# Who adds the residual in the last stages of a sandwich layer: GpSimd row by row, or VectorE in one instruction

## The chip, the cores and the metric

The kernel runs on one core of a Trainium2 chip. The metric is the device time of one execution in microseconds. Before the change it is 695.41 us, the median of three runs (694.97 to 696.55).

A core has five engines that each work off their own queue in order: TensorE (PE in the profile; its weight loads are listed as PEld), VectorE (DVE), ScalarE (ACT), GpSimd (POOL) and SyncE (SP), which here only issues DMAs. Engines wait for each other by semaphores. Matmuls write PSUM; everything else lives in SBUF, 128 partitions wide, and in DRAM.

## What is computed

Two residual layers over 8 sequences of 512 tokens with 256 features: linear attention, and a mixture of 8 experts of which each token uses 2. Each layer is normed on both sides. Cut to what matters here, the second one is:

```python
def ffn(x, ...):
    flat = x.reshape(-1, d)
    ... # top 2 of 8 experts, with their weights in combine
    out = 0.5 * gelu(flat @ shared_W + shared_b)
    for e in range(8):
        h = gelu(flat @ W1[e] + b1[e])
        out = out + combine[:, e:e + 1] * (h @ W2[e] + b2[e])
    out = (out - mean(out)) * rsqrt(var(out) + 1e-5) * gamma + beta
    return out

x = x + layernorm(attn(layernorm(x)))
x = x + layernorm(ffn(layernorm(x)))     # this last sum is what the change is about
```

All arithmetic is in fp32.

## The kernel before

**Fronts.** For each sequence a front (`front`) runs the attention layer, the first norm of the second layer, the shared expert and the choice of experts. It leaves three things in DRAM: the residual `x1_d`, the shared expert's output `acc_d`, and the token rows, scattered to their experts' slots.

**Jobs.** The experts' work is a list of jobs (`routed`), each a run of 128 to 512 slots of one expert. A job has a first layer (matmuls `ph`, L837; ScalarE's Gelu `h`, L844), and a second one (matmuls `po`, L959, for each tile of 128 slots; VectorE adds the bias, L962, and multiplies by the token's weight, L966, into `y`). GpSimd then issues an indirect DMA that adds the 128 rows of `y` to `acc_d` (`add_rows`, L812). Jobs of 512 slots, a wide first layer, use seven products in place of eight (L879), with sums before (VectorE's `T`, L796; GpSimd's `S`, L809) and after (VectorE's `hw`, L905 to L912). The last two jobs are not scattered: their rows are gathered straight into the last sequence by matmuls (`fin`, L1045) and added by VectorE (L1049).

**Last stages.** When all of a sequence's rows are in `acc_d`, its last stage (`back`) brings it home. It is a generator of six steps, and a table (`plan`) written out by hand says after which piece of which job each step is issued:

1. SyncE loads `accb` from `acc_d` and `xb` from `x1_d`.
2. VectorE takes statistics of `accb` (`st_d`, L983; `mv_d`, L985), and GpSimd makes the factor `rs_d` (L365, L366).
3. VectorE norms `accb`, with gamma and beta (L989, L993).
4. VectorE takes statistics again (`st_e`, L375; `mv_e`, L377); GpSimd makes `rs_e` and `sh_e` (L365, L366, L381, L382, L998).
5. ScalarE applies them to `accb`, four instructions of 256 columns (L387), and GpSimd adds `accb` to `xb`, four more (L1008).
6. SyncE stores `xb` to the output.

The steps of sequences 0 to 2 lie under the jobs of 512 slots of experts 0 to 3, those of 3 and 4 under the later jobs of experts 4 to 7, those of 5 and 6 under the last jobs. The end is close: sequence 6's steps 5 and 6 and sequence 7's last ones are all issued after the same, last piece, in this order. Sequence 7 takes another way (`close`), which the change leaves as it is.

**Order.** TensorE, VectorE and ScalarE keep the order in which the program issues their work (`manual_schedule`). GpSimd's work and the DMAs that it issues are chained by `in_turn`, SyncE's DMAs by `move`. So each engine's queue is the program's order, and an instruction that waits holds all that stand behind it on its engine.

There is a second user of the helper `finish_rows`: a loop at the end of the program that recomputes tokens if the experts' slots overflow. With these inputs it doesn't run, and nor does the branch in front of it; all 28 instructions of L1008 in the trace belong to sequences 0 to 6.

Of the kernel before, what the change touches and what calls it, by code (L numbers as in the profile page):

```python
# [10 lines left out]
ALU = mybir.AluOpType  # L11
# [5 lines left out]
def kernel(  # L17
# [21 lines left out]
    nc = tc.nc  # L39
# [5 lines left out]
    NT = C // P  # L45
# [339 lines left out]
    def ln_apply(dst, src, stats, t):  # L385
        rs, sh = stats[0:2]
        nc.scalar.activation(  # L387
            dst, src, AF.Identity, scale=rs[:, t : t + 1], bias=sh[:, t : t + 1]
        )
# [584 lines left out]
            yield  # L974


    def finish_rows(tiles, xts, shift, name, on_pool):

        n = len(tiles)
        st = small.tile([P, NT, 6], F32, tag="st", name=f"st_d{name}", bufs=3)  # L980
        mv = small.tile([P, NT, 2], F32, tag="mvd", name=f"mv_d{name}", bufs=3)
        for t in range(n):
            nc.vector.bn_stats(st[:, t, :], tiles[t])  # L983
        for t in range(n):
            nc.vector.bn_aggr(mv[:, t, :], st[:, t, :])  # L985
        rs = rsqrt(mv[:, 0:n, 1], n, f"d{name}", 4.0 * LN_EPS)
        yield
        for t in range(n):
            nc.vector.scalar_tensor_tensor(  # L989
                tiles[t], tiles[t], mv[:, t, 0:1], fgam, ALU.subtract, ALU.mult  # L990
            )
        for t in range(n):
            nc.vector.scalar_tensor_tensor(  # L993
                tiles[t], tiles[t], rs[:, t : t + 1], fbet, ALU.mult, ALU.add
            )
        yield
        rs, sh, _ = ln_stats(tiles, f"e{name}")
        in_turn(nc.gpsimd.tensor_tensor(sh[:, 0:n], sh[:, 0:n], shift, ALU.add))  # L998
        yield
        for t in range(n):  # L1000
            if on_pool:
                in_turn(nc.gpsimd.tensor_scalar(
                    tiles[t], tiles[t], rs[:, t : t + 1], sh[:, t : t + 1], ALU.mult, ALU.add
                ))
                in_turn(nc.gpsimd.tensor_tensor(xts[t], xts[t], tiles[t], ALU.add))
            else:
                ln_apply(tiles[t], tiles[t], (rs, sh), t)
                in_turn(nc.gpsimd.tensor_tensor(xts[t], xts[t], tiles[t], ALU.add))  # L1008

    def back(b, in_order=True):  # L1010
        acc = act.tile([P, NT, D], F32, tag="acc", name=f"accb_{b}", bufs=4)
        last = len(adds)
        if in_order:
            first = [j[0:2] for j in jobs[: n_jobs - CLOSE] if j[1] < room(b, j[0])]
            last = max(ends[j] for j in first)
        ld = move(acc, rows_of(acc_d, b))
        unordered(ld, "acc", [fills[b], *adds[last - 1]])

        tag, bufs = ("acc", 4) if b < 3 else ("x", XB)
        xt = act.tile([P, NT, D], F32, tag=tag, name=f"xb_{b}", bufs=bufs)  # L1020
        move(xt, rows_of(x1_d, b))
        yield
        if b < B - 1 or not in_order:
            yield from finish_rows(
                [acc[:, t, :] for t in range(NT)], [xt[:, t, :] for t in range(NT)],
                shifts[:, b, :], f"{b}", False,
            )
            yield
            move(out[b].rearrange("(p t) d -> p t d", t=NT), xt)
        else:  # L1030
            yield from close(acc, xt)
# [319 lines left out]
    with tc.If(n_any > 0, preferred_fallthrough_block=False):  # L1351

        with tc.If(n_rest > 0, preferred_fallthrough_block=False):
            for k, y, one_w, _ in closing:
                nc.vector.tensor_scalar_mul(y, y, one_w)
                adds.append([add_rows(k, 0, y, adds[-1]).ins])
            jobs += [(E + m, CAP, CAP + P) for m in range(MORE, MOST)]
            for k in range(n_jobs, len(jobs)):
                biases_of(jobs[k][0] - E)
                load_w(jobs[k][0])  # L1360
                fetch(k)
                if k == n_jobs:
                    turn(k)
                fetch(k + 1)
                for _ in routed(k):
                    pass
            for _ in back(B - 1, in_order=False):
                pass

        out_flat = out.rearrange("b c d -> (b c) d")
        with tc.If(n_steps > 0, preferred_fallthrough_block=False):
            with tc.For_i(0, n_steps, 1) as u:
                xt = act.tile([P, NU, D], F32, tag="x", name="dx", bufs=XB)
                nc.sync.dma_start(
                    xt, x1_d[bass.ds(u * -U + (B * C - U), U), :].rearrange("(p t) d -> p t d", t=NU)
                )
                comb = small.tile([P, NU, E], F32, tag="wd", name="dcomb")
                nc.sync.dma_start(  # L1380
                    comb, comb_d[bass.ds(u * -U + (B * C - U), U), :].rearrange("(p t) e -> p t e", t=NU)
                )
                shift = small.tile([P, NU], F32, tag="sd", name="dshift")
                nc.sync.dma_start(
                    shift, shift_d[bass.ds(u * -U + (B * C - U), U), :].rearrange("(p t) o -> p (t o)", t=NU)
                )
                xn = act.tile([P, NU, D], F32, tag="xn", name="dxn", bufs=XN)
                stats = ln_stats([xt[:, t, :] for t in range(NU)], "dc")
                for t in range(NU):
                    ln_apply(xn[:, t, :], xt[:, t, :], stats, t)  # L1390
                xT = act.tile([P, ND, U], F32, tag="xT", name="dxT", bufs=4)
                transposed(xT, [xn[:, t, :] for t in range(NU)], "d")
                acc = act.tile([P, NU, D], F32, tag="y", name="dacc", bufs=2)
                for t in range(NU):
                    ps = bank(f"dpsh_{t}")[:, 0, :]
                    for i in range(ND):
                        nc.tensor.matmul(
                            ps, xT[:, i, t * P : (t + 1) * P], wsg[:, i, 0:D],
                            start=(i == 0), stop=(i == ND - 1),
                        )  # L1400
                    nc.vector.tensor_tensor(acc[:, t, :], ps, bsh, ALU.add)
                nc.scalar.activation(acc, acc, AF.Gelu)
                for e in range(E):
                    load_w(e, name="d")
                    hs = []
                    for c in range(NH):
                        ph = bank(f"dph_{e}_{c}")[:, 0, :]
                        for i in range(ND):
                            nc.tensor.matmul(
                                ph[:, 0:U], w1[e][:, i, c * P : (c + 1) * P], xT[:, i, :],  # L1410
                                start=(i == 0), stop=(i == ND - 1),
                            )
                        ht = act.tile([P, U], F32, tag="h", name=f"dh_{e}_{c}", bufs=10)
                        nc.scalar.activation(
                            ht, ph[:, 0:U], AF.Gelu, bias=cols[:, e * NH + c : e * NH + c + 1]
                        )
                        hs.append(ht)
                    for t in range(NU):
                        po = pair(f"dpo_{e}_{t}")[:, 0, 0:D]
                        for c in range(NH):  # L1420
                            nc.tensor.matmul(
                                po, hs[c][:, t * P : (t + 1) * P], w2[e][c],
                                start=(c == 0), stop=(c == NH - 1),
                            )
                        yd = act.tile([P, D], F32, tag="rT", name=f"dy_{e}_{t}", bufs=2)
                        nc.vector.tensor_tensor(yd, po, b2b[e], ALU.add)
                        nc.vector.scalar_tensor_tensor(
                            acc[:, t, :], yd, comb[:, t, e : e + 1], acc[:, t, :], ALU.mult, ALU.add
                        )
                for _ in finish_rows(  # L1430
                    [acc[:, t, :] for t in range(NU)], [xt[:, t, :] for t in range(NU)],
                    shift, "dd", True,
                ):
                    pass
                nc.sync.dma_start(
                    out_flat[bass.ds(u * -U + (B * C - U), U), :].rearrange("(p t) d -> p t d", t=NU), xt
                )
# [32 lines left out]
```

## Time and profile before

| What | Value |
|---|---|
| Median of 3 runs | 695.41 us |
| The profiled execution's own time | 696.92 us |
| Its span in the profile | 695.2 us |
| Mean granted clock of TensorE | 0.976 |
| VectorE, busy from 500 us on (of 196 us) | 127.94 us |
| GpSimd, busy from 500 us on | 96.14 us |
| L1008, GpSimd's residual adds | 28, of 722 to 1752 ns, median 1268 ns |
| First and last start of L1008 | 538.3 and 675.9 us |

Times in the profile count from the start of the span. A line of the timeline gives the start, the duration, the engine, the line of the program, the operation with output and inputs, and how many instructions were merged; in brackets stands how long the engine had been idle, and what released it. A line of the waits gives who waited for whom, the total in us, how many times, and the longest. TensorE's end times are modelled, and spans on GpSimd are rough.

The last stages' residual adds fall in these stretches of GpSimd: sequence 0 at 538.27 for 3.31 us, sequence 1 at 567.35 for 4.17, sequence 2 at 593.32 for 3.47, sequence 3 at 632.52 for 3.30, sequence 4 at 643.40 for 3.31, sequence 5 at 661.30 for 3.29, sequence 6 at 673.88 for 2.79. The stores follow at 541.61, 571.54, 596.82, 637.96 and 649.81 us for the first five.

### The profile page before, as it was taken

The numbers are of one execution on the slowest core, as the hardware profiler recorded it, in microseconds if no ns is written. First come the engines' busy times: TensorE is split into PE (matmuls) and PEld (weight loads), VectorE is DVE, ScalarE is ACT, GpSimd is POOL, SyncE is SP. The second block draws the span as 40 slices with busy tenths as digits, with TensorE's granted clock in tenths as the row PEclk, the third lists the DMA queues.
The fourth block names the chain that finished last, engine by engine and source line by source line (L and its number), as shares of the span: only waits on it lengthen the run. The fifth ranks groups of instructions, "written<-read, shape, count | busy, mean of one in ns | idle before, by whom it ended". The sixth has DMA issues, their size and how long they took to land. (4 is left out here: it accounts for less than half of the span.)

```text
span 695.2 us, 10360 instructions
## 1 busy us (share of the span) xinstructions
PE 652.5 (94%) x3387; PEld 571.5 (82%) x3387; DVE 374.0 (54%) x1226; ACT 239.9 (35%) x589; POOL 317.0 (46%) x445
## 2 busy tenths in 40 slices
PE   6998989998999999999999999999999999998980
PEld 4887877876988888999898888898988887888870
DVE  3657769774565441111126466353677978246475
ACT  4444443553353323222233132131414134223440
POOL 4312326776547772212144345242436572536562
PEclk9999998999999999999999999999999999999995
DMA  7996113242978859755455354262645649799641
GB/s 227 381 346 247 62 61 122 108 145 108 293 237 271 283 123 265 219 153 130 129 133 166 85 170 104 48 174 34 188 130 174 198 120 305 205 286 297 215 144 58
DMA packets 77817, 124.17 MB, mean 179 GB/s; under 512 B 10870, under 2 KB 55100, under 8 KB 77756
## 3 DMA queue, kind: packets, MB, share of 16 engines
q1 hardware_dynamic: 65324, 106.22, 46.3%
q0 software_dynamic: 12432, 17.21, 13.0%
q8 instruction: 29, 0.48, 0.3%
q14 instruction: 32, 0.26, 0.1%
HBM read 83.58 MB, written 39.83 MB: 178 GB/s over the span
## 5 line engine op out<-in xcount | busy, mean ns | idle before, releaser
L812 POOL DMA_INDIRECT acc_d<-y,xr x65 | 102.0, 1570 | 210.6 <-DVE y L966 169.9
L959 PE MATMUL po<-w,h 128*128 128x256 f32 x560 | 127.2, 383 | 2.8 <-ACT h L844 2.8
L837 PE MATMUL ph<-rT,w 128*128 128x128 f32 (+1 forms) x800 | 127.5, 317 | 0.0
L837 PEld LDWEIGHTS ph<-rT,w 128*128 128x128 f32 x800 | 116.5, 191 | 9.0
L959 PEld LDWEIGHTS po<-w,h 128*128 128x128 f32 x560 | 105.5, 192 | 16.7 <-ACT h L844 3.2
L959 PE MATMUL po<-w,hw 128*128 128x256 f32 x512 | 115.2, 382 | 0.0
L844 ACT ACTIVATE h<-ph,cols 128x128 f32<-128x128 f32 (+1 forms) x176 | 60.5, 414 | 142.5 <-PE ph L837 141.3
L959 PEld LDWEIGHTS po<-w,hw 128*128 128x128 f32 x512 | 95.3, 190 | 16.2 <-ACT hw L885 4.2
L962 DVE TENSOR_TENSOR y<-po,b 128x256 f32<-128x256 f32 x67 | 28.3, 422 | 149.1 <-PE po L959 148.8
L721 POOL DMA_INDIRECT xs<-xn,slot x64 | 65.1, 1017 | 21.4 <-issue 19.0
L879 PE MATMUL p<-T,S 128*128 128x256 f32 x192 | 52.2, 380 | 0.6 <-DVE hw L905 0.6
L885 ACT ACTIVATE hw<-hw,cols 128x512 f32<-128x512 f32 x64 | 42.7, 714 | 25.5 <-DVE hw L912 25.5
L408 DVE COPY rT<-pt_r 128x512 f32<-128x512 f32 (+2 forms) x22 | 10.5, 475 | 61.6 <-PE pt_r L397 61.6
L879 PEld LDWEIGHTS p<-T,S 128*128 128x128 f32 x192 | 36.3, 190 | 6.1 <-DVE hw L905 1.3
L900 ACT COPY p<-p 128x256 f32<-128x256 f32 x32 | 11.9, 372 | 84.5 <-PE p L879 84.5
L879 PE MATMUL p<-rT,w 128*128 128x256 f32 x128 | 38.1, 379 | 0.0
L608 PE MATMUL psh<-wsg,xfT 128*128 128x264 f32 x128 | 32.7, 413 | 0.0
L573 PE MATMUL py<-wm,xT 128*128 128x256 f32 x128 | 29.2, 380 | 1.7 <-DVE wm L564 1.5
L608 PEld LDWEIGHTS psh<-wsg,xfT 128*128 128x128 f32 x128 | 26.1, 207 | 4.7
L573 PEld LDWEIGHTS py<-wm,xT 128*128 128x128 f32 x128 | 23.8, 189 | 5.8 <-ACT acc L618 1.1
L905 DVE TENSOR_TENSOR hw<-p,p 128x512 f32<-128x512 f32 x32 | 22.1, 690 | 10.3 <-PE p L879 10.3
L879 PEld LDWEIGHTS p<-rT,w 128*128 128x128 f32 x128 | 24.3, 190 | 3.3
(222 smaller groups left out, 984.8 us busy)
## 6 DMA issues: line engine op xcount, KB each, us to landing
w<-in_L_ffn_W_dram SPq DMA_DIRECT2D x50, 1024.0 KB, 6.9
xs<-pad SPq DMA_DIRECT2D x8, 1060.0 KB, 15.4
xr<-xs SPq DMA_DIRECT2D x26, 265.0 KB, 3.0
x<-in_L_attn_x_dram SPq DMA_DIRECT2D x8, 512.0 KB, 4.5
x_d<-x SPq DMA_DIRECT2D x8, 512.0 KB, 2.9
acc_d<-acc SPq DMA_DIRECT2D x8, 512.0 KB, 2.7
accb<-acc_d SPq DMA_DIRECT2D x8, 512.0 KB, 4.3
xb<-x_d SPq DMA_DIRECT2D x8, 512.0 KB, 5.0
```

The costliest lines, as they stand in the source:

```text
L573: nc.tensor.matmul(py[:, t, :], xT[:, i, tt * P : (tt + 1) * P], wm[:, i, 0:D], start=(i == 0), stop=(i == ND - 1),)
L608: nc.tensor.matmul(ps[:, t, 0 : D + E], xT[:, i, tt * P : (tt + 1) * P], wsg[:, i, :], start=(i == 0), stop=(i == ND - 1),)
L721: ins = in_turn(nc.gpsimd.indirect_dma_start(out=xs[:, :], out_offset=bass.IndirectOffsetOnAxis(ap=slot[:, t, j : j + 1], axis=0), in_=row ...
L812: ins = in_turn(nc.gpsimd.indirect_dma_start(out=acc_d[:, :], out_offset=bass.IndirectOffsetOnAxis(ap=xrs[k][t][:, DX - 1 : DX].bitcast(I3 ...
L837: nc.tensor.matmul(ph[:, (c - c0) * cs : (c - c0 + 1) * cs], w1[e][:, i, c * P : (c + 1) * P], rT[:, i, :], start=(i == 0), stop=(i == ND ...
L844: nc.scalar.activation(ht, ph[:, (c - c0) * cs : (c - c0 + 1) * cs], AF.Gelu, bias=(cols[:, e * NH + c : e * NH + c + 1] if e < E else b1m ...
L879: nc.tensor.matmul(dst, s(g), t, start=True, stop=True)
L885: nc.scalar.activation(part, part, AF.Gelu, bias=cols[:, c : c + 1])
L900: nc.scalar.copy(p1, p15[:, 0, :])
L905: nc.vector.tensor_tensor(h[:, 0:4:3, :], p26, p1.unsqueeze(1).to_broadcast(shape2), ALU.add)
L959: nc.tensor.matmul(po, h[t], w2[e][c], start=(n == 0), stop=(n == NH - 1),)
L962: nc.vector.tensor_tensor(y[:, t % CT, :], po, b2b[e], ALU.add)
```

## The change

Step 5 loses GpSimd's four adds and ends with ScalarE's apply. Step 6 begins with one VectorE instruction that adds all 1024 columns of `accb` to `xb`, and the store waits for it. In the loop that doesn't run here, the apply moves from GpSimd to ScalarE and the add from GpSimd to VectorE.

```diff
-    def finish_rows(tiles, xts, shift, name, on_pool):
+    def finish_rows(tiles, shift, name):
...
         for t in range(n):
-            if on_pool:
-                in_turn(nc.gpsimd.tensor_scalar(
-                    tiles[t], tiles[t], rs[:, t : t + 1], sh[:, t : t + 1], ALU.mult, ALU.add
-                ))
-                in_turn(nc.gpsimd.tensor_tensor(xts[t], xts[t], tiles[t], ALU.add))
-            else:
-                ln_apply(tiles[t], tiles[t], (rs, sh), t)
-                in_turn(nc.gpsimd.tensor_tensor(xts[t], xts[t], tiles[t], ALU.add))
+            ln_apply(tiles[t], tiles[t], (rs, sh), t)
...
             yield from finish_rows(
-                [acc[:, t, :] for t in range(NT)], [xt[:, t, :] for t in range(NT)],
-                shifts[:, b, :], f"{b}", False,
+                [acc[:, t, :] for t in range(NT)], shifts[:, b, :], f"{b}"
             )
             yield
+            nc.vector.tensor_tensor(xt, xt, acc, ALU.add)
             move(out[b].rearrange("(p t) d -> p t d", t=NT), xt)
```

The instructions of TensorE and ScalarE keep their order. On VectorE the new instruction of each sequence stands where step 6 is issued. For sequences 0, 1 and 2 that is behind the third `y` (L962, L966) of the job under which it lies; for 0 and 1 the next sequence's `st_e` comes next. Sequence 3's stands right behind `mv_e` of sequence 4, sequence 4's behind the `y` of expert 6's last job. Sequence 5's stands between the `y` of the second last job and `st_e` of sequence 6. Sequence 6's stands behind its own `mv_e` and ahead of the first two L1049, the last job's picks and its `y`.

## Prediction

> **What bounds the kernel now.** I read the page's engine table first, then the chain of waits, then TensorE's waits from 500 us on (the last stages lie there), then the timelines around each residual add.
>
> ```profile
> PE 652.5 (94%) x3387; PEld 571.5 (82%) x3387; DVE 374.0 (54%) x1226; ACT 239.9 (35%) x589; POOL 317.0 (46%) x445
> ...
> PE po L959 <- ACT h L844: 2.8, 1, 2.8
> PE fin L1045 <- DVE y L962: 2.2, 2, 1.7
> PE p L879 <- DVE hw L905: 0.6, 1, 0.6
> ```
>
> TensorE is busy 94% of the span, and the chain of waits only covers the last 2.3 us, on VectorE. So the adds matter in three places only: the three waits of TensorE above (after 500 us it has no others of weight), and the tail after its last matmul, where VectorE alone sets the end. GpSimd's 46% is no limit by itself.
>
> **The price of an add.** VectorE's two-input adds out of SBUF: 422 ns for 256 columns (the T rows, L796), 692 ns for 512 (the xb row, L1083). Slope 270 ns for 256 columns, so 1024 columns: 692 + 2 x 270 = 1.23 us, and the next instruction starts about 0.08 us before it ends (L1083 started 685.60, its follower 686.21), so 1.15 us in a queue. Seven of them: 8.6 us of VectorE. They replace 28 GpSimd adds of 1.27 us median, in seven stretches of 2.8 to 4.2 us, 23.6 us together. Nothing waits for those sums but the stores; what counts is whom each engine keeps waiting.
>
> **Sequences 0 and 1** (expert jobs with wide first layers). VectorE stalls while GpSimd adds: L966 at 539.95 took 1.80 us instead of 0.35; in sequence 1 the four L989 at 567.38 took 3.56 us and the four L993 2.12 us, against 1.66 and 1.66 in sequence 0. Rebuilt from sequence 0's start-to-start times, VectorE goes from the first L989 to the first hw add of the next job in 8.55 us. Without GpSimd's adds, but with the new one (1.2 us) in that stretch, sequence 0 reaches hw at 540.2 + 8.55 + 1.2 = 549.95 (before: 550.21), sequence 1 at 567.38 + 8.55 + 1.2 = 577.1 (before: 578.18). TensorE waited there for hw, 0.2 us and 0.65 to 0.8 us. I take **-0.9 us**; bounds: nothing gained, and +1.2 us each if the stall stays.
>
> **Sequence 2.** The add comes ahead of a job with a narrow first layer; VectorE idles 2.6 us per output tile there (L962 waits for po). Nothing. Without that cover it would cost 1.15 us of VectorE.
>
> **SyncE's queue, sequences 0 to 2.** The store moves from GpSimd's end (541.6, 571.5, 596.8) to VectorE's add (about 547.6, 575.0, 600.6), and what is queued behind it moves too: the first-layer weights of experts 4, 5, 6 by 6, 3.4 and 3.8 us, and a dozen loads behind the second. Experts 4, 5, 6 use those weights at 601.8, 616.0 and 630.1, some 29 us or more after the new issue, and a 1 MB weight lands in 6.9 us; the nearest other user is the gathered rows for the job of 594.4, issued at 584.3, perhaps 3 us later, landing within 3 to 6 us. Nothing; at the other end some 2 us if the DMA engines, 0.9 to 1.08 busy from 600 to 636, pass it on.
>
> **Sequences 3 and 4: the recovered stall.**
>
> ```profile
> 631.00 5.11 DVE L989 SCALAR_TENSOR_TENSOR accb<-accb,mv_d,fgam 128x256 f32<-128x256 f32 x4
> ...
> 632.52 3.30 POOL L1008 TENSOR_TENSOR xb<-xb,accb 128x256 f32<-128x256 f32 x4
> ...
> 641.64 2.07 ACT L387 ACTIVATE accb<-accb,sh_e,rs_e 128x256 f32<-128x256 f32 x4 [6.28 <-POOL sh_e L998]
> ...
> 644.02 5.41 PE L959 MATMUL po<-w,h 128*128 128x256 f32 x16 [2.75 <-ACT h L844]
> ```
>
> And one microsecond of the table of windows, whose field after the five engines' busy times is the granted clock:
>
> ```profile
> 646.00:647.00 1.00, 1.00 (x3) 0.74 (x3) 0.00 (x0) 0.08 (x1) 0.72 (x2) 0.50 0.98 285
> ```
>
> Read downwards, GpSimd's adds for sequence 3 hold VectorE's fourth L989 of sequence 4 (3448 ns instead of 477), so sequence 4's mean and variance come 3.45 us late, GpSimd's shift after them, ScalarE's apply after that; the job's Gelus are queued behind the apply, and TensorE idles 2.75 us. Then its clock is 0.50, from 645.1 to 648.5, and 16 matmuls take 5.41 us instead of 3.62. Layer starts of these jobs lie 7.25 us apart (630.07, 637.32); the next came at 649.27, so this place costs 11.95 - 7.25 = 4.7 us.
>
> After: the L989s and what follows end 3.45 us earlier, mv_e at 635.85. There the new add of sequence 3 starts (its inputs are long there) and GpSimd wants to read mv_e. Here a rule speaks against the change. The rows: a GpSimd scalar op of 0.23 us took 0.42 to 0.91 us beside VectorE's two-input ops, so +0.7 at most. The Trainium skill, SBUF — State Buffer, "Who interferes with whom": a VectorE instruction with two SBUF inputs contends with a GpSimd instruction that reads SBUF, and the second to issue blocks until the first is through. By that, GpSimd waits 1.1 us for the add. The apply then starts 2.35 us later (as 639.29 to 641.64): 638.9 by the rows, 639.3 by the rule; ends 641.0 or 641.4; the first Gelu is ready 0.3 us later, and TensorE wants it at 641.27. Stall 0.05 or 0.45 us. I take the rule's, since the 3448 ns row shows such a block in full: recovered **S = 4.25 us**, ends 3.8 and 4.7. Next gates: expert 8's weights (asked for at 624.9) and the rows of the last jobs, released by an indirect add that itself goes out 3 us earlier. None looks late.
>
> **Sequence 4's add**: VectorE idles 9.4 us. Nothing.
>
> **Tail: sequences 5 and 6.**
>
> ```profile
> 668.73 0.42 DVE L962 TENSOR_TENSOR y<-po,b 128x256 f32<-128x256 f32 x1
> 669.06 1.40 DVE L375 BATCH_NORM_STATS2 st_e<-accb 128x6 f32<-128x256 f32 x4
> ...
> 670.65 1.27 DVE L1049 TENSOR_TENSOR accb<-fin,accb 128x512 f32<-128x512 f32 x2
> ...
> 673.20 2.07 ACT L387 ACTIVATE accb<-accb,sh_e,rs_e 128x256 f32<-128x256 f32 x4 [4.44 <-POOL sh_e L998]
> 673.88 2.79 POOL L1008 TENSOR_TENSOR xb<-xb,accb 128x256 f32<-128x256 f32 x4 [0.71 <-ACT accb L387]
> 674.68 0.42 DVE L962 TENSOR_TENSOR y<-po,b 128x256 f32<-128x256 f32 x1 [1.85 <-PE po L959]
> ...
> 675.16 1.99 PE L1045 MATMUL fin<-y,pick 128*128 128x256 f32 x8 [0.52 <-DVE y L962]
> ```
>
> Before, the adds of sequence 6 ran on GpSimd beside everything. In VectorE's new order, add 5 stands between the first y and st_e, and add 6 straight after mv_e, ahead of the two L1049, the picks, the second y, and so of the last fin matmuls. Add 6 must wait for ScalarE's apply, which needs GpSimd, which needs mv_e: a round trip inside an in-order queue. From st_d of sequence 6 (before 661.41; after 661.41 - 4.25 - 0.3 for an indirect add landing sooner = 656.9): GpSimd no longer holds rs_d, so L993 starts at +3.4 instead of +4.8, the first y at +5.9 = 662.8; add 5 at 663.15; st_e 664.3; mv_e done +1.67 = 665.97; apply +2.42 to 668.4, done 670.5; add 6 at 670.55; L1049 x2 671.7; picks 672.9; second y 673.8 to 674.25; fin at **674.3**. By TensorE's shift alone fin would be at 675.16 - 4.25 = 670.9: the round trip costs **3.4 us**, and fin starts 0.86 us earlier than before.
>
> **The clock after that wait.** TensorE now idles from the end of po (668.8) to 674.3: 5.5 us. The trace: 2.75 us of idling brought 3.4 us at 0.50; 1.67 us brought none. The Trainium skill, TensorE: Matmul & The Clock Gate, "Why this matters for your kernels", warns of gaps over about 3 us. By it all 1.99 us of fin run at half speed, +2.0; by the trace, where the slow stretch was 3.4 us long and may have begun inside the gap, +1.0 to +1.9. I take **+1.5**; ends 0 and 2.
>
> **Sum.** fin: -0.86 - 0.9 + 1.5 = -0.3 us; all behind it (the last sums, norms and store) is as before. Against the profiled execution, 696.92 us (span 695.2 and 1.7 around it): 696.6. The median is 695.41, lowest 694.97. The 1.5 us between may be the half-clock stretch: it depends on where the idle gap falls in the window (the clock gate page, Part 1: the 3.4 us window runs free). Then a median run has less to recover, and 696.6 stands; if the difference is something else, 695.41 - 0.3 = 695.1. I lean to the former: **696.2 us**, own range 694.3 to 697.6.
>
> **Rivals.**
> - *The round trip decides* (slower): the tail cost, 3.4 + 1.5 us, is paid in full and S is not got: a weight or a row load is next in line, or the apply still comes late. Net 4.9 - 0.9 - S, so slower by over 0.2% once S is under 2.6 us. With S = 1: 698.4. For: the cost in the tail follows from the order of the queue, the gain from a chain of four engines. Against: no wait on DMA shows in those jobs.
> - *Relief decides* (faster): clock not halved in the tail, the rows of sequence 6 landing 1 us sooner, no block of GpSimd at 635.9: -0.3 - 1.5 - 0.7 - 0.4 = -2.9, 693.3 with half of the profiled offset. For: each is within its bounds; against: all are needed.
> - *VectorE in the wide stages* (slower): the stalls at 539.95 and 567.38 have another cause; two adds of 1.2 us delay hw and TensorE, +2.4 instead of -0.9: 699. Against: VectorE's long instructions end with GpSimd's adds each time.
>
> **Chances.** Forecast 0.45, round trip 0.26, relief 0.19, wide stages 0.10. A change below 0.2% (1.4 us) can't be told from none here. Forecast's share: same 0.30, slower 0.11, faster 0.04; round trip: slower 0.24, same 0.02; relief: faster 0.16, same 0.03; wide: slower 0.08, same 0.02. So faster 0.20, same 0.37, slower 0.43. Range 693.3 to 699.8: the two outer cases' times, and a little over for two costs together.
>
> **What would show it.** L989 of sequence 4 at 1.7 us in all, with no TensorE wait and no 0.50 clock near 644; hw waits near 550 and 578 gone; add 6 waiting some 4 us for ScalarE's apply, fin waiting for y by 5 us, a clock of 0.50 in the last fin. An L989 still of 3 us, or fin not waiting, would prove me wrong.

## The result, and the profile after

The changed kernel takes 700.95 us (median of 8 runs), the kernel before 697.52 us (8 runs beside them): the ratio is 1.0047, with a 95% interval from 1.0025 to 1.0069. The change makes the kernel slower by 1.7 to 4.8 us. The forecast of 696.2 us, and its range up to 699.8, are missed; that the median of before is itself 2.1 us higher than in the first three runs explains part of the miss in us, but not that the forecast's sum of -0.3 us came out as +3.4. The profiled execution took 703.92 us (span 702.2), the longest of the eight.

The changed kernel's page, its row of busy times:

```profile
PE 652.4 (93%) x3387; PEld 571.3 (81%) x3387; DVE 373.3 (53%) x1233; ACT 240.5 (34%) x589; POOL 299.9 (43%) x417
```

And its waits of TensorE from 500 us on (who waited for whom, total us, times, longest):

```profile
PE fin L1038 <- DVE y L962: 5.9, 2, 5.5
PE po L959 <- ACT h L844: 3.1, 2, 2.9
PE pt_r L397 <- DMA xr<-xs: 1.5, 1, 1.5
```

VectorE and GpSimd are both less busy than before, and the kernel is slower: what counts is TensorE's waits. The wait for hw is gone as forecast. But three waits of weight stand where there were three before: one for the gathered rows is new, the one at po has moved, and the one at fin has grown. In the order of the timeline:

**A new wait for the gathered rows.** SyncE's queue and TensorE, first before, then after:

```profile
571.54 0.34 SPq L129 DMA_DIRECT2D out_dram<-xb  x1
...
584.33 6.83 SPq L129 DMA_DIRECT2D xr<-xs  x2
...
594.44 0.60 PE L397 MATMUL pt_r<-identd,xr 128*128 128x128 f32 x4
```

```profile
576.89 0.34 SPq L129 DMA_DIRECT2D out_dram<-xb  x1
...
590.48 0.93 SPq L129 DMA_DIRECT2D xr<-xs  x2
...
597.32 0.63 PE L397 MATMUL pt_r<-identd,xr 128*128 128x128 f32 x4 [1.54 <-DMA xr<-xs]
```

The store of sequence 1 goes out at 576.89 (before 571.54), directly behind VectorE's add, and the loads behind it move with it: the rows xr (the first of the two merged loads) from 584.33 to 590.48. Before, they landed 7.5 us after their issue, 2.6 us ahead of their use. Now they land 6.7 us after it, and TensorE asks for them at 595.8, only 5.3 us after it.

**The stall of sequence 4, gone.** VectorE, GpSimd and TensorE:

```profile
633.91 1.67 DVE L989 SCALAR_TENSOR_TENSOR accb<-accb,mv_d,fgam 128x256 f32<-128x256 f32 x4
...
638.67 1.19 DVE L1021 TENSOR_TENSOR xb<-xb,accb 128x1024 f32<-128x1024 f32 x1
...
638.93 1.03 POOL L365 TENSOR_SCALAR rs_e<-mv_e 128x4 f32<-128x4 f32 x1 [2.99 <-DVE mv_e L377]
...
644.37 3.72 PE L959 MATMUL po<-w,h 128*128 128x256 f32 x16 [0.19 <-ACT h L844]
```

The four L989 take 1.67 us instead of 5.11, the wait at po is 0.19 instead of 2.75 us, and the sixteen matmuls run at full clock. GpSimd's first op on mv_e does block beside the new add: it takes 1.03 us instead of 0.23 and ends 0.10 us behind the add.

**A stall of the same kind, one sequence later.** SyncE, GpSimd and VectorE before:

```profile
649.38 0.33 SPq L129 DMA_DIRECT2D xr<-xs  x1
...
650.56 1.57 POOL L812 DMA_INDIRECT acc_d<-y,xr  x1 [3.85 <-DVE y L966]
...
653.97 1.67 DVE L993 SCALAR_TENSOR_TENSOR accb<-accb,rs_d,fbet 128x256 f32<-128x256 f32 x4 [0.54 <-POOL rs_d L366]
```

GpSimd, VectorE, ScalarE and TensorE after; the last line is that of L812 from 500 us on, the 23 semaphore waits of GpSimd's queue for indirect adds (shortest, median and longest in ns):

```profile
642.61 1.66 POOL L812 DMA_INDIRECT acc_d<-y,xr  x1 [0.66 <-issue]
652.66 1.56 POOL L812 DMA_INDIRECT acc_d<-y,xr  x1 [8.39 <-DVE accb L989]
653.70 0.81 POOL L365 TENSOR_SCALAR rs_d<-mv_d 128x4 f32<-128x4 f32 x1
...
655.67 1.67 DVE L993 SCALAR_TENSOR_TENSOR accb<-accb,rs_d,fbet 128x256 f32<-128x256 f32 x4 [3.58 <-POOL rs_d L366]
...
661.35 2.07 ACT L387 ACTIVATE accb<-accb,sh_e,rs_e 128x256 f32<-128x256 f32 x4 [2.99 <-POOL sh_e L998]
...
663.73 1.99 PE L959 MATMUL po<-w,h 128*128 128x256 f32 x8 [2.88 <-ACT h L844]
...
L812 POOLq EVENT_SEMAPHORE  x23: 17/43/9499, 511.1 to 661.2; - x23
```

Expert 7's rows y are ready at 648.9 (before 650.3), but their indirect add is issued at 652.66. The program lets a job's indirect adds wait for those of the job before it (`done` in `add_rows`), and this one waits until expert 6's, issued at 642.61, has landed at 651.93: that is the queue's wait of 9.50 us, and SyncE's next load of rows, held by the same landing, goes out at 651.98. The name in the bracket, L989, is only the event that came last by the profile; the adds do not read what L989 writes. Behind the add in GpSimd's queue stands rs_d of sequence 5, whose input was ready at 650.5. So VectorE idles 3.58 us before L993 instead of 0.54, sequence 5's chain comes 3.0 us late, its apply stands ahead of the second last job's Gelus, and TensorE waits 2.88 us.

Before, the same landing let SyncE's load go at 649.38, 0.9 us ahead of expert 7's rows, so their add had nothing to wait for. The landing hardly moves when the add is issued sooner. Counted from the first layer of expert 4's last job, the add was issued 40.5 us on in the four executions without sequence 3's change (before, e12, e1, e3) and landed 47.5 to 47.8 us on; in the eleven with it, it was issued 37.9 us on and landed 46.2 to 47.2 us on. Issued 2.6 us sooner, it landed 0.9 us sooner in the mean.

**The tail.** VectorE and TensorE, and two microseconds of the table of windows (the field after the five engines is the granted clock):

```profile
676.88 1.23 DVE L1021 TENSOR_TENSOR xb<-xb,accb 128x1024 f32<-128x1024 f32 x1 [4.52 <-ACT accb L387]
678.03 1.28 DVE L1042 TENSOR_TENSOR accb<-fin,accb 128x512 f32<-128x512 f32 x2
...
680.61 3.78 PE L1038 MATMUL fin<-y,pick 128*128 128x256 f32 x8 [5.47 <-DVE y L962]
```

```profile
678.00:679.00 1.00, 0.00 (x0) 0.00 (x0) 1.00 (x3) 0.45 (x2) 0.00 (x0) 1.00 0.05 20
...
681.00:682.00 1.00, 1.00 (x3) 0.78 (x3) 0.00 (x0) 0.00 (x0) 0.00 (x0) 0.50 0.00 0
```

The round trip is as forecast: add 6 stands 4.52 us in VectorE's queue waiting for ScalarE, everything behind it with it, and fin starts late, at half clock.

**The sum in the two traces.** From the first layer of expert 4's last job (601.78 before, 604.70 after) to the end of VectorE's last instruction it is 85.96 us before and 90.27 after: +4.31. In it are -4.26 (the first layer behind the recovered stall 43.23 us on instead of 47.49), +3.11 (from there to the last first layer: 17.63 instead of 14.52), +3.68 (from that to the last fin: 15.05 instead of 11.37) and +1.78 (from there to the end). Ahead of that stretch are -0.94 for sequences 0 and 1 and +1.54 for xr: +4.9 in all. VectorE ends 7.2 us later in all; of the 2.3 us left, 2.1 lie in the front, where nothing is changed.

### The profile page after: what moved, and what is told of

Its sections match the earlier page's. It is cut to its first block, busy times and chain, and to the rows that moved or that the text cites. A ratio compares the mean times of both kernels' runs of the same rounds, so it can differ in the third digit from the quotient of the medians.

```text
span 702.2 us, 10331 instructions
## 1 busy us (share of the span) xinstructions
PE 652.4 (93%) x3387; PEld 571.3 (81%) x3387; DVE 373.3 (53%) x1233; ACT 240.5 (34%) x589; POOL 299.9 (43%) x417
## 5 line engine op out<-in xcount | busy, mean ns | idle before, releaser
L812 POOL DMA_INDIRECT acc_d<-y,xr x65 | 104.4, 1606 | 221.1 <-DVE y L966 167.2
L962 DVE TENSOR_TENSOR y<-po,b 128x256 f32<-128x256 f32 x67 | 28.3, 422 | 140.7 <-PE po L959 140.7
L573 PE MATMUL py<-wm,xT 128*128 128x256 f32 x128 | 30.9, 396 | 3.9 <-DVE over L673 2.2
L608 PE MATMUL psh<-wsg,xfT 128*128 128x264 f32 x128 | 29.9, 387 | 0.0
L608 PEld LDWEIGHTS psh<-wsg,xfT 128*128 128x128 f32 x128 | 24.1, 191 | 3.9
```

Source lines behind the costliest of these rows:

```text
L573: nc.tensor.matmul(py[:, t, :], xT[:, i, tt * P : (tt + 1) * P], wm[:, i, 0:D], start=(i == 0), stop=(i == ND - 1),)
L608: nc.tensor.matmul(ps[:, t, 0 : D + E], xT[:, i, tt * P : (tt + 1) * P], wsg[:, i, :], start=(i == 0), stop=(i == ND - 1),)
L812: ins = in_turn(nc.gpsimd.indirect_dma_start(out=acc_d[:, :], out_offset=bass.IndirectOffsetOnAxis(ap=xrs[k][t][:, DX - 1 : DX].bitcast(I3 ...
L962: nc.vector.tensor_tensor(y[:, t % CT, :], po, b2b[e], ALU.add)
```

## The experiments

Every ratio is against the kernel before, on the same chip. What the profiles give is told as single executions.

**Where in the sequences is the loss?** Three kernels keep GpSimd's adds for all sequences but some (`ON_POOL` names those that keep them):

```diff
+    ON_POOL = (0, 1, 2, 3, 4, 5)      # e1;  e2: (0, 1, 2, 4, 5, 6);  e3: (3, 4, 5, 6)
...
-            nc.vector.tensor_tensor(xt, xt, acc, ALU.add)
+            if b not in ON_POOL:
+                nc.vector.tensor_tensor(xt, xt, acc, ALU.add)
```

e1, sequence 6 alone:

> Only sequence 6's add is on VectorE, the other six stay on GpSimd. Round trip theory (VectorE waits for ScalarE's apply ahead of the last job's work): fin starts 3.9 us later (y at 669.15, mv_e 670.7, apply done 675.3, add 6, two L1049, picks, y: 679.05 against 675.16) and its matmuls run at half clock, +1.5 to 1.8: +5.4 to 5.7 us, a ratio to before of 1.0078 (1.006 to 1.009), more than the whole change. Rival (the loss comes from VectorE's extra work in the wide jobs, the tail hides its own): within 1 us of before.

Measured: 1.0081 (1.0059 to 1.0103). fin waits 4.27 us for y and then takes 3.78 us. By the medians the tail alone costs more than the whole change; the two intervals overlap.

e2, sequence 3 alone:

> Only sequence 3's add is on VectorE. Theory that the recovered stall moves on to sequence 5 because an indirect add lands late: the L844 stall near 644 shrinks from 2.75 us to 0.5 or less and the slow clock behind it goes, a stall of 2 to 3 us shows up some 16 us later, net -1 to -2 us, ratio 0.997 to 0.999. Rival (the stall is got back in full and only the tail gives it away in the changed kernel): -4.3 us, ratio 0.994. Second rival (GpSimd's adds do not hold VectorE): no change, with L989 still over 3 us.

Measured: 0.999 (0.997 to 1.0011). L989 is at 1.67 us, the stall of sequence 4 gone, and a new one stands in the trace:

```profile
652.64 3.72 PE L959 MATMUL po<-w,h 128*128 128x256 f32 x16 [0.19 <-ACT h L844]
671.31 3.64 PE L959 MATMUL po<-w,h 128*128 128x256 f32 x8 [2.19 <-ACT h L844]
```

With nothing but sequence 3's add changed, the recovered stall comes back one sequence later, here with a half clock too (3.64 us for 8 matmuls instead of 1.99). So relief that shows in full at its own place in the trace is hardly seen in the time.

e3, sequences 0 to 2 alone:

> Only sequences 0, 1 and 2 have their adds on VectorE. Theory: TensorE's waits for hw near 550 and 578 go, -0.9 us; the store of sequence 1, now later, holds a dozen loads, and the rows for expert 4's second job come late, +1.5 us: net +0.6 us, ratio 1.000 to 1.002, with a wait of pt_r for xr of 1 to 2 us. Rival (VectorE's extra work in the wide jobs is the loss): +2.4 us or more, 1.0035, with longer waits for hw.

Measured: 1.0 (0.9975 to 1.0025). The waits for hw are gone, and TensorE waits 1.47 us for xr: gain and cost in the same place.

**The tail, by moving the step.** e4 is the changed kernel with step 6 of sequence 6 a piece later, so behind the last y:

```diff
-    ... (6, (7, 9, 10, 11, 13, 13)), ...
+    ... (6, (7, 9, 10, 11, 13, 14)), ...
```

> The changed kernel with one number of the plan altered: step 6 of sequence 6 is issued one piece later, behind the last job's y, where VectorE waits 1.2 us for fin anyway. Round trip theory: fin no longer waits 5.5 us for y and runs at full clock, -5.5 us against the changed kernel, so 2 us below before, ratio 0.997 (0.995 to 0.999). Rival (the tail is not the cause): as the changed kernel, 1.0047.

Measured: 0.9984 (0.9963 to 1.0006), 0.6% under the changed kernel. fin's wait is 0.52 us, at full clock. What remains: waits of 2.73 us at po, of 1.68 for xr and of 1.57 at the first fin (before 1.67), and add 6, which now stands ahead of the last sums:

```profile
679.75 1.23 DVE L1021 TENSOR_TENSOR xb<-xb,accb 128x1024 f32<-128x1024 f32 x1 [1.59 <-ACT accb L387]
680.89 1.28 DVE L1042 TENSOR_TENSOR accb<-fin,accb 128x512 f32<-128x512 f32 x2
```

**The tail, by undoing it.** e10 is the changed kernel with sequence 6's adds back on GpSimd (`ON_POOL = (6,)`):

> The changed kernel with one part undone: the adds of sequence 6 back on GpSimd, in four parts at their steps of before; sequences 0 to 5 stay on VectorE. Theory (the round trip of add 6 through VectorE and ScalarE before the last y costs 3.7 us and the clock that falls in it 1.8 us, and add 6 also stands ahead of the last L1042s, 1.5 us): the wait for y before fin L1038 falls from 5.5 to under 1 us, fin L1038 takes about 2 us and not 3.8, and the time is 5.5 to 7 us under the changed kernel's: ratio to before about 0.9965. The wait of 2.8 us for h (L844) at po of sequence 5 and that of 1.5 us for xr stay. Rival (the loss of the changed kernel is in the adds of sequences 0 to 5): ratio as the changed kernel's, 1.0047.

Measured: 0.9964 (0.9949 to 0.998), as expected. TensorE's waits:

```profile
PE po L959 <- ACT h L844: 2.5, 2, 2.3
PE fin L1044 <- DVE y L962: 1.2, 2, 0.7
PE pt_r L397 <- DMA xr<-xs: 1.1, 1, 1.1
```

Undoing this one part turns the loss into a gain: without the tail the change is worth 2.5 us (1.4 to 3.6).

**The stall of sequence 5, by moving a step.** e5 (with e4's edit) issues sequence 5's statistics and rs_d a piece earlier, ahead of expert 7's indirect add; e6 (with e4's edit) issues its apply a piece later, behind the Gelus:

```diff
-    ... (5, (2, 5, 6, 7, 9, 11)), ...
+    ... (5, (2, 4, 6, 7, 9, 11)), ...     # e5
+    ... (5, (2, 5, 6, 7, 10, 11)), ...    # e6
```

> As e4, and the statistics of sequence 5 (step 2) are issued one piece earlier, so that on GpSimd its rs_d stands ahead of the indirect add of expert 7's last job. Theory (that add waits for the one before it to land, 9 us after its issue, and holds rs_d behind it on GpSimd, so the apply of sequence 5 comes late and holds the Gelus): the wait of po for h near 663 falls from 2.7 us to 0.3 or less, -2.5 us against e4, ratio to before 0.995. Rival (the apply is late for another reason: the load of accb, or ScalarE's own work): the wait stays over 2 us, ratio as e4, 0.998.

> As e4, and the apply of sequence 5 (step 5) is issued one piece later, behind all eight Gelus of its job on ScalarE, with its cause left as it is. Theory (the harm of a late apply is that Gelus are queued behind it): the wait of po for h near 663 goes, -2.7 us against e4, ratio to before 0.995, while rs_d of sequence 5 stays as late as in e4. Rival (something else holds the Gelus or po): no change from e4, 0.998.

Measured: e5 0.9977 (0.996 to 0.9994), e6 1.0001 (0.9985 to 1.0017). In both the stall at po is gone. In e5 the first fin waits 3.76 us in its place (1.57 in e4), and runs at half clock:

```profile
662.71 1.66 POOL L812 DMA_INDIRECT acc_d<-y,xr  x1 [3.50 <-DMA acc_d<-y,xr]
665.07 1.41 DVE L983 BATCH_NORM_STATS2 st_d<-accb 128x6 f32<-128x256 f32 x4 [7.26 <-DMA accb<-acc_d]
671.43 3.78 PE L1038 MATMUL fin<-y,pick 128*128 128x256 f32 x8 [3.76 <-DVE y L962]
```

Now it is sequence 6's load of acc_d that VectorE waits for, and that load waits for expert 7's indirect add. In e6 the first fin waits 1.70 us, about as long as in e4 and before, and a wait of 0.67 us for rT is new; from expert 4's last job to the last fin its trace is 1.9 us shorter than e4's, but the time shows no gain (on another chip), and why isn't settled. Two later pairs of kernels differ in e6's edit alone: from e7 to e8 and from e13 to e11 a wait of 2.3 to 2.4 us at po goes, and one of 2.0 to 2.1 us at the first fin comes, where there was none. So moving steps of sequence 5 passes the delay on; both expectations took it for a local one.

**The store of sequence 1.** e7 (with e4's edit) issues the stores of sequences 0 and 1 five pieces later, e9 (with e4's edit) that of sequence 1 alone; the add stays where it is:

```diff
             nc.vector.tensor_tensor(xt, xt, acc, ALU.add)
+            if b == 1:                    # e7: if b < 2
+                yield
             move(out[b].rearrange("(p t) d -> p t d", t=NT), xt)
...
         for n in (0, 1, 3, 4, 8, 10):
             at(*under[6 * b + n], b)
+        if b == 1:                        # e7: if b < 2
+            at(*under[6 * b + 15], b)
```

> As e4, and the stores of sequences 0 and 1 leave step 6 and are issued five pieces after their adds, so that SyncE has no store ahead of the weights and rows of the next jobs. Theory (the store that waits for VectorE's add holds those loads): the wait of pt_r for xr near 597 goes, -1.6 us against e4, ratio to before 0.996. Rival (the rows come late since the weights' transfers take long, whatever the order): the wait stays at 1 us or more, ratio as e4.

> The kernel of e4 (step 6 of sequence 6 a piece later), with the store of sequence 1 alone issued five pieces later; the store of sequence 0 stays where it is. Theory (the store of sequence 1 waits in SyncE's queue for VectorE's add and holds the loads of the gathered rows behind it): TensorE's wait of 1.7 us for xr at L397 is gone, 1.6 us less than e4, ratio to before about 0.996. Rival (the rows land late for another reason: traffic, or the indirect adds): a wait of 1 us or more for xr stays, ratio about 0.998 as in e4.

Measured: e7 1.0007 (0.9989 to 1.0024), e9 0.9956 (0.9937 to 0.9974). e7 doesn't answer the question: with store 0 moved behind it, the load of xb for sequence 2 takes a buffer that waits 16.4 us in SyncE's queue for VectorE's add of sequence 1, so the rows came late all the same (TensorE waited 2.31 us). In e9 the rows go out at 581.94, 9.8 us ahead of their use, and TensorE's waits are

```profile
PE po L959 <- ACT h L844: 2.0, 2, 1.8
PE fin L1040 <- DVE y L962: 0.7, 2, 0.5
```

No wait for xr, with the same load landing 7.0 us after its issue: it was the store in SyncE's queue that made the rows late. The ratio falls from e4's 0.9984 to 0.9956, but on another chip and with intervals that overlap, so what the wait cost in time is rough, some 2 us.

**Together.** e8 is e4, e6 and e7 in one; e11 has sequence 6 on GpSimd, e6's later apply and e9's later store; e13 is e11 without the later apply:

> All three together: add 6 a piece later, apply of sequence 5 a piece later, the stores of 0 and 1 later. If the three costs are separate, -5.5 - 2.7 - 1.6 us against the changed kernel and so 6 to 6.5 us below before: ratio 0.991 (0.989 to 0.993). If what is freed at one place is held at the next again, 0.994 to 0.997 with a new wait of TensorE after 660.

> Three parts together: the adds of sequence 6 on GpSimd as before, the others on VectorE; the apply of sequence 5 a piece later; the store of sequence 1 five pieces later. If the three costs are separate (tail 5.5 us, po of sequence 5 2.8 us, xr 1.5 us, and the gains of 0.9 and 4.25 us stay): ratio to before 0.991 to 0.995, faster than both kernels. If one cause stands behind the other (the stall of sequence 5 passes on to fin, as in e5 and e6): about 0.998, with a new wait of TensorE for y or rT in place of the ones removed.

> Two parts together: the adds of sequence 6 on GpSimd as before (e10), and the store of sequence 1 five pieces later (e9); sequence 5 stays as in the changed kernel. If the two costs are separate: TensorE's wait for xr is gone, fin starts without a long wait, ratio to before 0.994 to 0.9955, faster than both kernels, and faster than e11; the wait of about 2 us for h at po of sequence 5 stays. If taking the wait for xr away only lengthens the wait for h at po: 0.9964 as in e10.

Measured: e8 1.0017 (0.9999 to 1.0034), e11 0.9965 (0.9943 to 0.9986), e13 0.9954 (0.9931 to 0.9976). e8 carries e7's flaw (2.91 us for xr) and missed both of its expectations. e11 missed its range: the stall at po is gone, and in its place stands

```profile
663.30 3.63 PE L1046 MATMUL fin<-y,pick 128*128 128x256 f32 x8 [2.02 <-DVE y L962]
```

the delay passed on. e13 came as expected, though its interval overlaps e11's, so that e13 is the better of the two isn't shown. e9 and e13 are both faster than the kernel before and than the changed one: 0.45% under before.

**The common cause.** If expert 6's indirect add is the limit that is passed on, leaving it out must free both places. e14 is e13 without it, so 128 rows are missing from its sum:

```diff
-            ins = add_rows(k, t, y[:, t % CT, :], done)
-            mine.append(ins.ins)
+            if (e, s0) == (6, HELD + P):
+                mine += done
+            else:
+                ins = add_rows(k, t, y[:, t % CT, :], done)
+                mine.append(ins.ins)
```

> The kernel of e13 without the indirect add of the last job of expert 6 into acc_d: these 128 rows are missing from the sum. Theory (expert 7's indirect add waits in GpSimd's queue until expert 6's has landed, some 9 us after its issue, and holds rs_d of sequence 5; sequence 6's load of acc_d comes behind it): GpSimd's wait of about 8 us ahead of expert 7's indirect add goes, rs_d of sequence 5 comes 2 us earlier or more, the wait of about 2 us for h at po goes, and no new wait for y of its size comes at fin: 1.5 to 2.5 us under e13, ratio 0.990 to 0.993. Rival (the stall of sequence 5 has another cause, or passes on to fin): ratio within 0.001 of e13.

Measured: 0.9901 (0.9862 to 0.994), beside e13's 0.9954 on the same chip: about 3.7 us less. The intervals overlap a little, but five of e14's six executions are below the shortest of e13's fifteen (696.64 us). In e13, GpSimd and TensorE:

```profile
644.33 1.66 POOL L812 DMA_INDIRECT acc_d<-y,xr  x1 [0.66 <-issue]
653.87 1.56 POOL L812 DMA_INDIRECT acc_d<-y,xr  x1 [7.88 <-DVE accb L989]
...
664.93 3.47 PE L959 MATMUL po<-w,h 128*128 128x256 f32 x8 [2.37 <-ACT h L844]
...
L812 POOLq EVENT_SEMAPHORE  x23: 17/43/8994, 514.5 to 662.4; - x23
```

and in e14:

```profile
651.55 1.66 POOL L812 DMA_INDIRECT acc_d<-y,xr  x1 [7.28 <-DVE y L966]
652.95 0.74 POOL L365 TENSOR_SCALAR rs_d<-mv_d 128x4 f32<-128x4 f32 x1
...
L812 POOLq EVENT_SEMAPHORE  x22: 17/42/43, 515.1 to 660.4; - x22
```

with all that TensorE waits for after 500 us:

```profile
PE fin L1049 <- DVE y L962: 0.5, 1, 0.5
PE po L959 <- ACT h L844: 0.2, 1, 0.2
```

The queue's wait of 9 us is gone, expert 7's add waits only for its own rows, and TensorE waits 0.7 us altogether. Leaving the add out spares its transfer too; that the queue's wait goes with it ties the stall to the landing. The gain is more than the 1.5 to 2.5 us expected; in the traces the stretch from expert 4's last job to the end is 4.0 us shorter, of which 2.4 are the wait and some 1.6 the half clock that followed it in e13's execution.

**The control.** e12 is the kernel before once more:

> The kernel before, unchanged, as a control on the same chip: ratio 1.000 within 0.002. If the stages ahead of any changed instruction differ between executions of one kernel, the time at which expert 4's last job starts its first layer differs from the 601.8 us of the first profile by some us, while the stretch from there to the last fin L1038 stays 73.4 us within 1 us. If that stretch itself varies by 2 us or more, differences of that size between single traces of two kernels mean nothing.

Measured: 1.0004 (0.9987 to 1.0021). Expert 4's last job starts at 600.47 us instead of 601.78, and from there to the last fin it takes 73.38 us, to the hundredth what it took in the first profile. So the last stretch can be compared between single traces, all but the clock (e1 and e3 have the same wait at po and run on at full speed), and the front cannot: over all profiles that start lies between 599.07 and 613.02.

## Why the prediction was wrong, step by step

Two steps that were put at nothing failed: "None looks late" behind the recovered stall (3.11 us) and "Nothing" for SyncE's queue (1.54 us). Every other term of the sum came within 0.3 us.

- **The price of an add**, 1.23 us: measured 1.19 to 1.23. Right.
- **Sequences 0 and 1, -0.9 us**: -0.94 between the two traces. Right.
- **SyncE's queue, "Nothing"**: wrong, +1.54 us. The right user was named, the gathered rows for the job of 594.4, with two terms too small. They were to be issued "perhaps 3 us later": it was 5.0 (590.48 - 584.33 = 6.15, less the 1.18 by which TensorE is late there). And they were to land "within 3 to 6 us": it was 6.7, and in the trace of before this very load had taken 7.5, with 2.6 us to spare; the profile's median for such loads, 3.0, hides it. The cost lies within the forecast's own outer end of some 2 us, but for another reason than the one given there. e9 shows that the store is the cause.
- **Sequences 3 and 4, S = 4.25 us**: 4.26 at its own place, with the block of GpSimd that the rule foretold (its op ends with VectorE's add). But 1.8 of it is half clock that the profiled execution happened to have: e12 has it too (5.38 us for the sixteen matmuls), e1 and e3 have the same wait of 2.76 us and take 3.72. A typical run may have less to recover; how often isn't known.
- **"None looks late"**: the step that failed most, +3.11 us. It named the right resource, the rows "released by an indirect add that itself goes out 3 us earlier". Expert 6's add did go out 2.6 us earlier against TensorE's work, but it took 9.3 us instead of 7.1 and landed only 0.3 us earlier; expert 7's rows came 4.3 us earlier and found it not yet landed. So expert 7's add waits, in GpSimd's in-order queue, with rs_d of sequence 5 behind it. The trace of before had the numbers: SyncE's load at 649.38 marks the landing, and rs_d of sequence 5 started 1.4 us behind the add ahead of it, so not before 650.8 as long as the landing stays where it was; the forecast's own shift asked for it at 651.97 - 4.25 = 647.7. e2 shows that the recovered stall alone brings the new one, e14 that it goes with expert 6's add.
- **The round trip, +3.4 us**: 3.68 against TensorE's own shift (the last fin waits 4.95 us longer, the first one 1.28 less). Right in kind and nearly in size. **The clock, +1.5**: 1.78, as all eight matmuls ran at half clock (3.78 us instead of 1.99).
- **The sum**: -0.3 forecast; with the four misses (1.54 + 3.11 + 0.28 + 0.28 = 5.2) it is the +4.9 of the two traces. The medians say +3.4, within 1.7 to 4.8. The excess of the single traces isn't settled; the half clock of the tail, 1.8 us in this execution, would be enough for it if other executions don't have it.
- **The rivals**: "The round trip decides" named the direction, and why S might not be got, "a weight or a row load is next in line"; and its time with S = 1, 698.4, is nearer than the forecast's. With this rival slower was, at 0.43, the likeliest of the three outcomes; the central time still sat near no change. It doubted the gain for "a chain of four engines", and the chain had a fifth member, a DMA.

## What to carry to other kernels

When a stall is taken away, follow the stage that now runs earlier until it meets a time that doesn't move with it: here the landing of a DMA issued by another job, one queue further on. An instruction that waits for another engine's answer does not belong in the middle of an in-order queue: put it behind the work that TensorE is waiting for, or leave it on the engine that has nothing else to do. And when work moves from one engine to another, the store that follows it moves too, with all the loads behind it; compare each load's lead with its landing time, not with the mean.

## What the runs showed of the hardware

- Indirect adds of 128 rows of 256 fp32 took from 3.7 to 9.4 us from issue to landing in the kernel before (median 4.6). Expert 6's took 9.3 us in the changed kernel and 7.1 before, and landed at nearly the same point of TensorE's work. The windows of the changed kernel from 643 to 650 us show the DMA engines at a share of 0.81 to 1.10, then 0.71, and 0.14 at 651, when it lands; before, they show 0.98 at 646, 0.49 at 647, 0.07 at 648, and it lands at 649.3. Whether that traffic is the cause wasn't tried.
- The same idle gap of TensorE, 2.75 to 2.76 us, was followed by half clock in two executions (5.41 and 5.38 us for sixteen matmuls) and by full clock in two others (3.72). Gaps of 2.02 us (e11), 2.19 (e2) and 2.37 (e13) were followed by 3.63, 3.64 and 3.47 us for eight, one of 2.88 (the changed kernel) by 1.99. Over all profiles, of twelve gaps of 2.0 to 2.9 us before po or fin five were followed by a slow clock; of seven of 1.5 to 1.9 us none, of three of 3.7 us or more all. Between 2 and 3 us the length of the gap alone doesn't decide.
- One 1.19 us add on VectorE stretched a GpSimd op of 0.23 us to 1.03 us; four GpSimd adds in a row stretched a VectorE instruction of 0.48 us to 3.45 us (the kernel before, at 632.7).
